# A graph-attention layer on one core: V's slice with its first two score blocks together, another order of V's products, and row statistics at other slots

## The chip, the core and the metric

The kernel runs on one core of one Trainium2 chip. The metric is the device time of one execution in microseconds; the time given for a kernel is the median of its runs. One further execution was recorded by the hardware profiler, and all rows of a profile below come from such a recorded execution.

The engines are named as the profile names them: PE is TensorE's matmuls, PEld its weight loads, DVE is VectorE, ACT is ScalarE, POOL is GpSimd, and SP is the engine from whose queue nearly all transfers are issued.

## The reference

All values are fp32. x is 128 graphs of 128 nodes with 768 features, and adj holds 128 x 128 edge weights per graph, about seven of eight of them zero.

```python
h = relu(layernorm(x))                      # over the 768 features
q, k, v = (split_heads(h @ W + b) for W, b in ((Wq, bq), (Wk, bk), (Wv, bv)))   # 12 heads of 64
scores = q @ k.T / sqrt(64) + beta * adj
scores = where(adj > 0, scores, -9e15)
out = x + merge_heads(softmax(scores) @ v)
```

Each of the 128 graphs attends within itself.

## The kernel before

**Groups and slices.** The graphs go in 32 groups G of four (`GRP`, `NG`). Each group needs three matrix products with the activations of its four graphs: one for Q and K of heads 0 to 5 ("qk0"), one for V ("v"), one for Q and K of heads 6 to 11 ("qk1"). For group 0 they are done plainly (`plain_slice`); for groups 1 to 31 each is a *slice* of 15 products (`slice_z`), by a fast scheme for multiplying 3 x 3 blocks in two rows, and each of the 15 is itself done with seven block products instead of eight (`ZONES`). The loop over G (L1068) writes the work of the three slices into a table `todo` by slot, and `run` (L807) then plays a slice: slot k is the k-th product in the order of `ORDER`. Every engine's instructions run in the order in which this program writes them; nothing reorders them later.

**One product (`product_z`, L531).** It takes 28 matmul instructions (two passes for each of 14), which read one weight tile `T_...` or resident `res_...` and one sum of activations, and write one pair of PSUM banks. There are four pairs. `PRODUCTS` (L66) gives each product a *chain* a, b, c or d. Products of one chain add up in the same pair of banks, in their order, and after each product the pair's content so far is added to one or two results, called homes, named (r, j). So the next product of a chain may write only when the last one's content has been read. A chain takes its pair at its first product and gives it back at its last. For the first products in question:

| product | chain | result (r, j) |
|---|---|---|
| 1 | a | (1, 0), first use |
| 0 | c | (1, 1), first use |
| 3 | b | (1, 0) |
| 5 | a | (0, 0), first use |
| 2 | c | (0, 1), first use |
| 7 | b | (0, 0) |
| 10 | a | (0, 2), first use |
| 6 | c | (0, 2) |
| 13 | a | (1, 2), first use |
| 4 | d | (1, 1) and (1, 2) |
| 8 | d | (1, 0) |

**Reading a pair ("drain").** In V's slice a result's first use is read by VectorE for two of seven blocks (L561) and then ScalarE for five (L562); any later use is one VectorE addition of all seven (L571). After the last use GpSimd turns the home into V's rows (`decode`, L581).

**Scores (L617).** `scores(G, u, j)` writes the scores of two heads for four graphs: 32 matmuls in tiles of another shape (64 x 64), into a pair of its own. It sets its two homes free. At the next slot VectorE adds the mask (L634) and gives the pair back; ScalarE takes the exponential (L636) behind that slot's drain.

**A slot.** `run` writes, in this order: the product's matmuls, then the next weight load (`load_T`, L330, on SP; five buffers, the tile just used is refilled for the fifth streamed product after it); pending masks; the slot's table entries (`then(at, ...)`); what falls due from earlier slots; the product's drain; pending exponentials and divisions; and last the slot's "post" entries.

**Row statistics.** Layernorm's mean and variance of group G+2 are taken while group G is computed, graph by graph (g = 0 to 3): `load_row` (L408) brings the 384 KB of a graph, `row_stats` (L411) sums it and its squares on ScalarE, writing over the buffer (L417 to L419). From group 3 on there is one buffer (`row_home`), so a load waits for the statistics before it, on SP, and all transfers that SP issues later stand behind that wait. The next group's activations are normalised by ScalarE (`norm`, L446, "post" at slots 3, 4, 7, 8 of V's slice), transposed by VectorE (`to_hT`, L459; A11 at slot 10), and summed.

**The order of V's slice before**, with the tables of the change: products 1, 0, 3, 5, 2, 7, 10, 6, 11, 13, 4, 9, 14, 8, 12, in chains a c b a c b a c b a d c b d c. Scores of (u, j) = (0, 2) are at slot 0, (0, 1) at slot 2, (0, 0) at slot 7. Row statistics of g = 1, 2, 3 stand behind slots 1, 5 and 10, the loads of g = 2 and 3 behind slots 2 and 6. In groups 30 and 31 V's slice has no row statistics.

Of the kernel before, what the change touches and what calls it, by code (L numbers as in the profile page):

```python
# [30 lines left out]
@with_exitstack  # L31
def kernel(
    ctx: ExitStack,
    tc: tile.TileContext,
    x: bass.AP,
    adj: bass.AP,
    wq: bass.AP,
    bq: bass.AP,
    wk: bass.AP,
    bk: bass.AP,  # L40
    wv: bass.AP,
    bv: bass.AP,
    beta: bass.AP,
    out: bass.AP,
):

    nc = tc.nc
    keep = ctx.enter_context(tc.tile_pool(name="keep", bufs=1))
    bad = keep.tile([1, 1], I32, name="bad")
    args = (x, adj, wq, bq, wk, bk, wv, bv, beta, out)
    direct(tc, *args, bad)
    again = nc.values_load(bad[0:1, 0:1])
    with tc.If(again > 0):
        general(tc, *args)
# [48 lines left out]

ZORDER = (1, 0, 3, 5, 2, 7, 10, 6, 11, 13, 4, 9, 14, 8, 12)
QORDER = (4, 0, 1, 8, 2, 3, 5, 6, 7, 10, 9, 11, 13, 12, 14)  # L110
LORDER = (1, 4, 0, 8, 5, 2, 10, 3, 6, 7, 13, 9, 11, 12, 14)
ORDER = {"qk0": ZORDER, "v": ZORDER, "qk1": QORDER}
RING = 5
RESIDENT = (3, 8, 12, 16, 20, 25, 29, 33, 35, 38, 41)

# [10 lines left out]
def direct(ctx, tc, x, adj, wq, bq, wk, bk, wv, bv, beta, out, bad):  # L126
# [132 lines left out]

    sequence = [(sl, n) for sl in ("qk0", "v", "qk1") for n in ORDER[sl]]  # L260
    resident = {key: const.tile([P, 7, P], F32, name=f"res_{key[0]}_{key[1]}") for key in (sequence[at] for at in RESIDENT)}
# [61 lines left out]
    def order_of(G, sl):  # L323
        return LORDER if G == NG - 1 and sl == "qk1" else ORDER[sl]

# [135 lines left out]
    def sum_acts(G, name):  # L461
        _, a, b, sign = [row for row in SUMS_A if row[0] == name][0]
        t = full[G, name] = block(SPOT.index(name))
        nc.vector.tensor_tensor(t, full[G, a], full[G, b], ALU.add if sign > 0 else ALU.subtract)
# [66 lines left out]
    def product_z(G, sl, n):  # L531
# [21 lines left out]
        for (r, j), sign in uses:  # L553
# [19 lines left out]
            if not left[key]:  # L573
                last = order_of(G, sl) is LORDER
                engine = nc.vector if sl == "qk1" and (n == 13 or last and n in (11, 12, 14)) else nc.gpsimd
# [240 lines left out]
    def slice_z(G, sl, todo):  # L816
        run([product_z(G, sl, n) for n in order_of(G, sl)], todo)
# [163 lines left out]
    def then(at, f, *args):  # L981
        todo.setdefault(at, []).append(lambda: f(*args))

    def bias(G, *at):
        def go():
            if G not in steps:
                steps[G] = bias_steps(G)
            next(steps[G], None)
        for n in at:
            then(n, go)  # L990

    def attention(G, u, at, behind=5):
        for n, j in at:
            then(n - 3, load_xo, G, 3 * u + j)
            then((n, "post"), attend, G, 3 * u + j, behind)
# [6 lines left out]
    def turn_act(G, slots, behind=0):  # L1002
        for at, name in slots:
            then(at, to_hT, G, int(name[1]), int(name[2]))
            if behind is not None:
                then(at + behind, inner, G, name)

    def sums_at(G, slots):
        for at, name in slots:
            then(at, sum_acts, G, name)  # L1010
# [57 lines left out]
    for G in range(1, NG):  # L1068
        more = G + 1 < NG
        todo.clear()  # L1070
        then(3, scores, G - 1, 1, 2)
        then(5, scores, G - 1, 1, 0)
        then((6, "post"), scores, G - 1, 1, 1)
        attention(G - 1, 1, ((7, 2), (10, 0), (12, 1)))
        sums_at(G, ((0, "S7"), (1, "S0"), (4, "S5"), (7, "S14"), (9, "S11")))
        if G == 1:
            todo[0].insert(0, lambda: sum_acts(1, "S6"))
        if more:
            for g in range(2):
                for h in range(2):  # L1080
                    then((2 * g + h, "post"), norm, G + 1, g, 2 * h, 2 * h + 2)
            turn_act(G + 1, ((8, "A01"), (9, "A00"), (11, "A02")), None)
            then((12, "post"), load_x, G + 1, 1)
            if G + 2 < NG:
                then((7, "post"), row_stats, G + 2, 0)
                then((9, "post"), load_row, G + 2, 1)
        slice_z(G, "qk0", todo)

        todo.clear()
        then(0, scores, G, 0, 2)  # L1090
        then(2, scores, G, 0, 1)
        then(7, scores, G, 0, 0)
        if more:
            then((11, "post"), add_raw, G + 1)
            for n, at in enumerate((3, 4, 7, 8)):
                then((at, "post"), norm, G + 1, 2 + n // 2, n % 2 * 2, n % 2 * 2 + 2)
            turn_act(G + 1, ((10, "A11"),), 1)
            for at, name in ((4, "A01"), (5, "A00"), (6, "A02")):
                then(at, inner, G + 1, name)
            if G + 2 < NG:  # L1100
                for g, at in ((1, 1), (2, 5), (3, 10)):
                    then((at, "post"), row_stats, G + 2, g)
                    if g < 3:
                        then((at + 1, "post"), load_row, G + 2, g + 1)
        slice_z(G, "v", todo)

        todo.clear()
        if not more:
            break
        attention(G, 0, ((3, 2), (9, 1)))  # L1110
        attention(G, 0, ((12, 0),), 6)
        turn_act(G + 1, ((1, "A10"), (4, "A12")), 1)
        sums_at(G + 1, ((6, "S1"), (7, "S9"), (8, "S2"), (11, "S6"), (13, "S10")))
        bias(G + 1, 0, 2, 4)
        if G + 2 < NG:
            then(5, row_moments, G + 2, 6, 9)
            then((6, "post"), load_x, G + 2, 0)
        if G + 3 < NG:
            then((10, "post"), load_row, G + 3, 0)
        slice_z(G, "qk1", todo)  # L1120
# [158 lines left out]
```

## Time and profile before

| | |
|---|---|
| median of three runs | 2706.36 us (2702.01 to 2708.77) |
| the profiled execution | 2712.82 us |
| its span, first to last instruction | 2711.0 us |
| mean granted TensorE clock | 0.996 |
| V's slice, groups 1 to 29, shortest and longest | 26.48 and 30.43 us |
| moved over the span | 721.73 MB, mean 266 GB/s |

The page of the profile gives shares of the span by engine, the chain of work that ended last, and the costliest groups of instructions. The timeline lists instructions in order of time; PE's durations overlap, since a matmul's end is modelled to the end of its pipeline, so the pace of PE is read from one start to the next.

### The profile page before, as it was taken

What the parts mean: (1) busy time and instruction counts of PE and PEld (TensorE: products, weight loads), DVE (VectorE), ACT (ScalarE), POOL (GpSimd) and SP (SyncE); (2) the same over time, 40 slices, a digit from 0 to 9 for tenths busy, and PEclk for the clock granted to TensorE, in tenths of its full rate; (3) what the DMA queues carried; (4) which work ended last, traced back from release to release, by engine and by line L of the source; (5) the groups of instructions that cost most, each with busy time, mean ns of one, the idle gap of its engine ahead of it and who ended that gap; (6) DMA issues with size and microseconds to landing.
All of it is one profiled execution on the core that took longest, in us unless ns stands there. A gap on an engine that the chain in (4) does not pass through costs nothing.

```text
span 2711.0 us, 121562 instructions
## 1 busy us (share of the span) xinstructions
PE 2674.2 (99%) x52029; PEld 2568.3 (95%) x52029; DVE 2188.4 (81%) x2705; ACT 1762.5 (65%) x4612; POOL 2096.0 (77%) x3034
## 2 busy tenths in 40 slices
PE   8999999999999999999999999999999999999997
PEld 7799999999999999999999999999999999999997
DVE  6878888788888788888788878788887888877885
ACT  2476666677666677666767666776666776667653
POOL 4867878777878877888778787778787778887783
PEclk9999999999999999999999999999999999999999
DMA  8789889899889898889899889898898988888875
GB/s 229 262 260 278 274 271 274 259 281 276 271 264 281 260 287 272 271 278 277 259 277 276 275 274 268 269 273 269 270 283 260 280 272 269 280 269 256 253 235 158
DMA packets 530342, 721.73 MB, mean 266 GB/s; under 512 B 105980, under 2 KB 374024, under 8 KB 529800
## 3 DMA queue, kind: packets, MB, share of 16 engines
q1 hardware_dynamic: 528640, 713.12, 86.4%
q8 instruction: 412, 6.75, 1.0%
q10 hardware_dynamic: 1160, 0.79, 0.1%
q14 instruction: 130, 1.06, 0.1%
HBM read 647.73 MB, written 66.05 MB: 263 GB/s over the span
## 4 chain that ended last, share of the span: by engine, by line
PE 87%; POOL 4%; DVE 3%; ACT 2%; DMA 1%; issue 1%; POOLq 0%; DVEq 0%; ACTq 0%
PE pair L547 74%; PE pair L626 7%; PE pair L683 6%; DMA sbig<-in_x_dram 1%; DVE home L571 1%; POOL home L590 1%; POOL home L589 1%; POOL home L592 1%; ACT sbig L419 0%; POOL home L591 0%; ACT sbig L417 0%; ACT home L562 0%; DVE e L634 0%; DVE prep_v L304 0%; ACT e L636 0%
## 5 line engine op out<-in xcount | busy, mean ns | idle before, releaser
L571 DVE TENSOR_TENSOR home<-home,pair 128x896 f32<-128x896 f32 x810 | 860.2, 1075 | 234.2 <-PE pair L547 130.4
L547 PE MATMUL pair<-sbig,T_qk 128*64 128x128 f32 x13888 | 888.6, 274 | 4.1 <-ACT e L666 3.1
L547 PEld LDWEIGHTS pair<-sbig,T_qk 128*64 128x64 f32 x13888 | 758.0, 137 | 17.8 <-issue 8.0
L666 ACT ACTIVATE e<-e,sm 128x64 f32<-128x64 f32 x1512 | 382.2, 341 | 123.5 <-DVE sm L654 123.2
L547 PE MATMUL pair<-A,T_qk 128*64 128x128 f32 x6076 | 415.1, 273 | 0.0
L547 PE MATMUL pair<-T_v,sbig 128*64 128x128 f32 x6944 | 414.2, 274 | 0.3 <-ACT home L562 0.3
L589 POOL TENSOR_TENSOR home<-home 128x256 f32<-128x256 f32 x297 | 227.2, 765 | 237.0 <-DVE home L571 237.0
L683 PE MATMUL pair<-v,e 128*64 128x65 f32 x6048 | 401.8, 221 | 0.0
L565 ACT ACTIVATE home<-pair 128x640 f32<-128x640 f32 x325 | 229.2, 705 | 261.5 <-PE pair L547 196.8
L547 PEld LDWEIGHTS pair<-T_v,sbig 128*64 128x64 f32 x6944 | 385.4, 137 | 6.3 <-issue 4.3
L683 PEld LDWEIGHTS pair<-v,e 128*64 128x64 f32 x6048 | 359.5, 137 | 3.6 <-DVE e L634 0.3
L547 PEld LDWEIGHTS pair<-A,T_qk 128*64 128x64 f32 x6076 | 331.7, 137 | 5.5 <-issue 5.5
L634 DVE SCALAR_TENSOR_TENSOR e<-pair,biasT 128x1024 f32<-128x1024 f32 x189 | 230.4, 1219 | 82.1 <-PE pair L626 82.0
L592 POOL TENSOR_TENSOR home<-home 128x256 f32<-128x256 f32 x297 | 276.3, 930 | 23.3
L590 POOL TENSOR_TENSOR home<-home 128x256 f32<-128x256 f32 x297 | 250.1, 842 | 23.3
L636 ACT ACTIVATE e<-e 128x1024 f32<-128x1024 f32 x189 | 200.2, 1059 | 64.7 <-DVE e L634 56.7
L446 ACT ACTIVATE x<-x,block 128x192 f32<-128x192 f32 x480 | 231.7, 540 | 0.0
L692 ACT ACTIVATE sm<-pair,tiny 128x8 f32<-128x8 f32 x189 | 49.3, 261 | 261.6 <-PE pair L683 261.6
L591 POOL TENSOR_TENSOR home<-home 128x128 f32<-128x128 f32 x297 | 196.9, 663 | 23.3
L547 PE MATMUL pair<-sbig,res_qk 128*64 128x128 f32 x3472 | 211.9, 273 | 0.0
L567 ACT ACTIVATE home<-pair,bqk 128x128 f32<-128x128 f32 x650 | 203.6, 374 | 0.0
L626 PE MATMUL pair<-home 64*64 64x128 f32 x5312 | 196.2, 277 | 6.3 <-issue 4.8
(192 smaller groups left out, 4699.9 us busy)
## 6 DMA issues: line engine op xcount, KB each, us to landing
T_qk<-kept_qk SPq DMA_DIRECT2D x713, 448.0 KB, 4.8
T_v<-kept_v SPq DMA_DIRECT2D x341, 448.0 KB, 4.9
xo<-in_x_dram SPq DMA_DIRECT2D x189, 256.0 KB, 4.5
out_dram<-xo SPq DMA_DIRECT2D x189, 256.0 KB, 5.9
x<-in_x_dram SPq DMA_DIRECT2D x248, 192.0 KB, 6.6
sbig<-in_x_dram SPq DMA_DIRECT2D x116, 384.0 KB, 6.5
kept_qk<-prep_qk SPq DMA_DIRECT2D x23, 448.0 KB, 2.9
adj<-in_adj_dram SPq DMA_DIRECT2D x128, 64.0 KB, 3.9
```

The source lines that it names most:

```text
L446: nc.scalar.activation(t, t, AF.Relu, bias=shift[G, n], scale=rstd[G, n])
L547: nc.tensor.matmul(p[q:q + HD, at, :], lhs[:, q:q + HD], rhs, start=(first and at % 4 == 0), stop=True, skip_group_check=True)
L565: nc.scalar.activation(t[:, 0:5], p[:, 0:5], AF.Copy, scale=float(sign))
L567: nc.scalar.activation(t[:, at], p[:, at], AF.Identity, bias=bqk[:, of, oc:oc + 1], scale=float(sign))
L571: nc.vector.tensor_tensor(t, t, p[:, 0:7], op)
L589: e.tensor_tensor(t[:, 1:4:2], t[:, 1:4:2], twice(5), ALU.add)
L590: e.tensor_tensor(t[:, 2:5:2], t[:, 2:5:2], twice(1), ALU.add)
L592: e.tensor_tensor(t[:, 0:7:6], t[:, 0:7:6], twice(2), ALU.add)
L626: nc.tensor.matmul(ps[k:k + HD, i, g * N:(g + 1) * N], keys[r, k:k + HD], queries[r], start=True, stop=True)
L634: nc.vector.scalar_tensor_tensor(e, ps, SCORE_CAP * ISCALE, bias, op0=ALU.min, op1=ALU.add)
L666: nc.scalar.activation(o[:, r, b, 0:HD], pa[:, r, b, 0:HD], AF.Copy, scale=t[:, 1, r, b:b + 1])
L683: nc.tensor.matmul(pa[q:q + HD, 2 * g + i, :], k[:, q:q + HD], vt[G, "v", r, h // 4][:, 4 * g + h % 4, :], start=True, stop=True, skip_gro ...
```

## The change

Three edits. V's slice gets an order of its own, in which product 3 goes from slot 2 to slot 4, and products 5 and 2 each come one slot sooner; its chains are then a c a c b b a c b a d c b d c. The score block (0, 2) goes from slot 0 to slot 2, where it is written ahead of (0, 1). The statistics of graphs 1 and 2 of group G+2 go from behind slots 1 and 5 to behind slots 4 and 6 (those of graph 3 stay at 10); the load of graph 2 goes from behind slot 2 to behind slot 4, and that of graph 3 from 6 to 7. The same weight tiles stay resident, since the products at those places are the same.

```diff
 ZORDER = (1, 0, 3, 5, 2, 7, 10, 6, 11, 13, 4, 9, 14, 8, 12)
 QORDER = (4, 0, 1, 8, 2, 3, 5, 6, 7, 10, 9, 11, 13, 12, 14)
+VORDER = (1, 0, 5, 2, 3, 7, 10, 6, 11, 13, 4, 9, 14, 8, 12)
...
-ORDER = {"qk0": ZORDER, "v": ZORDER, "qk1": QORDER}
+ORDER = {"qk0": ZORDER, "v": VORDER, "qk1": QORDER}
...
         todo.clear()
-        then(0, scores, G, 0, 2)
+        then(2, scores, G, 0, 2)
         then(2, scores, G, 0, 1)
         then(7, scores, G, 0, 0)
...
             if G + 2 < NG:
-                for g, at in ((1, 1), (2, 5), (3, 10)):
+                for g, at in ((1, 4), (2, 6), (3, 10)):
                     then((at, "post"), row_stats, G + 2, g)
                     if g < 3:
-                        then((at + 1, "post"), load_row, G + 2, g + 1)
+                        then((at + (g == 2), "post"), load_row, G + 2, g + 1)
         slice_z(G, "v", todo)
```

## The prediction

> **What bounds the kernel now.** I read the page first: the share of the span by engine, then the chain that ended last.
>
> ```profile
> span 2711.0 us, 121562 instructions
> PE 2674.2 (99%) x52029; PEld 2568.3 (95%) x52029; DVE 2188.4 (81%) x2705; ACT 1762.5 (65%) x4612; POOL 2096.0 (77%) x3034
> PE 87%; POOL 4%; DVE 3%; ACT 2%; DMA 1%; issue 1%; POOLq 0%; DVEq 0%; ACTq 0%
> ```
>
> TensorE is the bound: whatever makes it wait adds to the time, and what the other engines do is free as long as it lies under its matmuls. So I went on to the timeline of one V slice on each engine. The columns are start, duration, engine, line, operation, tiles and count; in brackets the idle time before and what ended it.
>
> ```profile
> 1312.59 1.70 PE L547 MATMUL pair<-T_v,sbig 128*64 128x128 f32 x28
> 1314.22 1.10 PE L626 MATMUL pair<-home 64*64 64x128 f32 x32
> 1315.26 1.75 PE L547 MATMUL pair<-res_v,sbig 128*64 128x128 f32 x28
> 1316.84 1.70 PE L547 MATMUL pair<-T_v,sbig 128*64 128x128 f32 x28
> ...
> 1332.28 1.75 PE L547 MATMUL pair<-res_v,A 128*64 128x128 f32 x28 [0.51 <-DVE e L634]
> ...
> 1338.54 1.70 PE L547 MATMUL pair<-res_v,A 128*64 128x128 f32 x28
> 1340.07 1.70 PE L547 MATMUL pair<-A,T_qk 128*64 128x128 f32 x28
> ```
>
> A product is one row of 28 matmuls and takes 1.53 us (1338.54 to 1340.07); a block of scores is a row of 32 and takes 1.04 us (1314.22 to 1315.26), with 0.10 us ahead of it (1312.59 + 1.53 = 1314.12) and 0.05 behind it (1315.26 to 1316.84 is 1.58). This slice lasts 27.48 us. One wait stands in it: product 4, at slot 10, waits 0.51 us for the mask of the third block.
>
> The same slice of every group with row statistics (groups 1 to 29), cut from its first product to the next slice's, stands in the view of windows (length, busy time and count of PE, PEld, DVE, ACT and POOL, then granted clock, DMA share, GB/s).
>
> ```profile
> 1890.40:1916.88 26.48, 26.48 (x522) 25.45 (x518) 18.56 (x23) 18.36 (x40) 21.76 (x37) 1.00 0.91 272
> 2466.00:2496.43 30.43, 28.57 (x520) 27.29 (x518) 18.91 (x23) 18.55 (x40) 21.90 (x37) 0.94 0.91 251
> sum 786.89, PE 776.32 PEld 740.98 DVE 539.20 ACT 534.60 POOL 626.92; mean PE 26.77 PEld 25.55 DVE 18.59 ACT 18.43 POOL 21.62
> ```
>
> An undisturbed slice takes 26.48 us; the mean is 786.89 / 29 = 27.13 us. So V's slices hold at most 0.65 us each, 19 us in all, that a better order could take back, beside what the change does to the matmuls themselves.
>
> **The change, part by part.** Times are now counted from the first matmul of V's slice. Slot k is the k-th product.
>
> *One entry into scores less.* Two blocks in a row share one 0.10 us ahead and one 0.05 us behind: 0.15 us saved, less what one block costs behind another (0 to 0.10 us); I take 0.10 us a group. Slots 0, 1, 2 start at 0, 1.53, 3.06; the scores run from 4.69 to 6.77; slot 3 starts at 6.82.
>
> *Chain a at slots 0 and 2 (before: 0 and 3).* A product adds to the pair of banks that its chain's last product was drained from, so it waits for that drain. The last slice shows what it costs to come two slots after: its fourth product stands two behind the one that shares its chain.
>
> ```profile
> 2663.24 1.70 PE L547 MATMUL pair<-sbig,T_qk 128*64 128x128 f32 x28
> 2665.84 0.44 PE L547 MATMUL pair<-A,res_qk 128*64 128x128 f32 x4 [0.90 <-ACT home L567]
> ```
>
> There the drain is longer. V's slot 0 is drained by VectorE and then ScalarE, which ends at 1314.87 + 0.71 - 1312.59 = 2.99 (row below); from the mask's end to the waiting product was 0.06 us (1331.00 + 1.22 = 1332.22 against 1332.28, next fence). So slot 2 could start at 3.05, and PE gets there at 3.06. Cost nothing, hidden by slot 1's matmuls with no margin; the bounds are 0 and 0.4 us (if ScalarE comes late by the 0.38 us it idles there now). I take 0. Chain c, at 1 and 3, has the two blocks between: nothing.
>
> *Chain b at slots 4 and 5 (before: 2 and 5).* This is the first real cost. Product 3 is now drained while nothing but product 7 is queued on PE, and product 7 is of the same chain.
>
> ```profile
> 1318.65 1.09 DVE L571 TENSOR_TENSOR home<-home,pair 128x896 f32<-128x896 f32 x1 [0.18 <-PE pair L547]
> ...
> 1321.37 0.42 DVE L561 TENSOR_TENSOR home<-bv_b,pair 128x256 f32<-128x256 f32 x1 [0.49 <-PE pair L547]
> ...
> 1330.00 1.09 DVE L571 TENSOR_TENSOR home<-home,pair 128x896 f32<-128x896 f32 x1 [3.63 <-ACT home L562]
> 1331.00 1.22 DVE L634 SCALAR_TENSOR_TENSOR e<-pair,biasT 128x1024 f32<-128x1024 f32 x1
> ...
> 1334.22 0.71 DVE L459 STREAM_TRANSPOSE A<-x 128x512 f32<-128x512 f32 x1 [0.68 <-ACT x L446]
> 1334.86 5.04 DVE L571 TENSOR_TENSOR home<-home,pair 128x896 f32<-128x896 f32 x5
> ```
>
> Product 3's own drain of before starts 1.81 us after its product (1316.84 to 1318.65) and takes 1.09; with 0.06 to PE that is 2.96 us, against 1.53 of product: 1.43 us of PE idle in each of 31 groups. VectorE is free for it: the second mask ends near 8.2, slot 3's part near 9.1, and slot 4 is done only at 10.2. Slot 5 starts at 8.35 + 2.96 = 11.31. Undisturbed, the slice now takes 26.48 - 0.10 + 1.43 = 27.8 us, its slot 13 starts 3.06 before the end, at 24.7.
>
> *Row statistics at 4, 6, 10 instead of 1, 5, 10; loads at 4 and 7 instead of 2 and 6.* All groups 3 and up share one row buffer, so this is a ring: statistics, load, statistics. ScalarE's timeline of before has the prices, and SP's the load.
>
> ```profile
> 1314.87 0.71 ACT L562 ACTIVATE home<-pair 128x640 f32<-128x640 f32 x1 [0.38 <-DVE home L561]
> ...
> 1319.13 0.83 ACT L417 ACTIVATE sbig<-sbig 128x768 f32<-128x768 f32 x1
> ...
> 1321.82 0.70 ACT L562 ACTIVATE home<-pair 128x640 f32<-128x640 f32 x1 [0.47 <-DVE home L561]
> 1322.42 1.05 ACT L636 ACTIVATE e<-e 128x1024 f32<-128x1024 f32 x1
> 1323.37 0.98 ACT L446 ACTIVATE x<-x,block 128x192 f32<-128x192 f32 x2
> 1324.24 0.69 ACT L562 ACTIVATE home<-pair 128x640 f32<-128x640 f32 x1
> ...
> 1327.14 0.84 ACT L417 ACTIVATE sbig<-sbig 128x768 f32<-128x768 f32 x1 [1.34 <-DMA sbig<-in_x_dram]
> ...
> 1329.28 0.68 ACT L562 ACTIVATE home<-pair 128x640 f32<-128x640 f32 x1
> ```
> ```profile
> 1321.37 0.33 SPq L409 DMA_DIRECT2D sbig<-in_x_dram  x1
> ```
>
> Now row 1 starts at 6.54 and its successor's load is issued at 8.78 (2.24 us later). In the new order ScalarE does, from slot 3 on: its drain, which starts 0.45 us behind VectorE's start (1321.37, 1321.82), and that 1.87 us behind the second product of a pair begun at 1319.50, so at 6.82 + 2.32 = 9.14; then 0.60 drain, two exponentials of 0.95, two pairs of norms of 0.87, and 2.24 of row 1: the load of row 2 goes out at 9.14 + 0.60 + 1.90 + 1.74 + 2.24 = 15.6, 6.9 us later than now. Row 2's statistics stand only two slots on, and ScalarE reaches them at 16.3, behind slot 6's drain.
>
> How long the load takes from issue to its reader: 5.77 us here, where ScalarE waited for it (1321.37 to 1327.14). The undisturbed group bounds it from the other side.
>
> ```profile
> 1903.47 0.84 ACT L417 ACTIVATE sbig<-sbig 128x768 f32<-128x768 f32 x1
> ```
> ```profile
> 1899.14 0.33 SPq L409 DMA_DIRECT2D sbig<-in_x_dram  x1
> ```
> ```profile
> L335 SPq DMA_DIRECT2D T_v<-kept_v x7: 319/323/392, 1312.8 to 1329.8; - x7
> ...
> DMA to landing us min/median/max: 3.3/4.9/6.6
> ```
>
> There it took at most 4.33 us, with no wait. The fastest of the larger weight transfers (448 KB against 384) landed in 3.3. In the new place SP itself stands at this load's wait from about 10.0 to 15.6, so what it issued earlier has landed and the load goes out alone: I take 3.8 us, between 3.3 and 4.33; the bounds are 3.3 and 5.8.
>
> Then everything behind it on ScalarE is late: row 2 starts at 19.4; 2.14 to its successor (1327.14 to 1329.28), norms 0.87, the third exponential 0.95, norms 0.87: 24.3. VectorE's transpose of A11 needs these norms and stands ahead of slot 10's two drains: 0.04 + 0.64, then two of 1.01 (5.04 for five), then 0.06 to PE: 27.1. Slot 13 (product 8) is of product 4's chain, d, and waits for both. PE is there at 24.7: **2.4 us of stall**, and the slice ends at 27.1 + 3.06 = 30.2. The formula is 26.4 plus the load's time; the cover is gone from 1.4 us of load time on, and no row is that short.
>
> SP's queue: slot 6's weight load waits from 14.4 to 15.7, and those of slots 8, 9 and 11 stand behind row 3's load, which waits for row 2 until 21.7. With five buffers they are the next slice's first three, due at 30.2: some 6.9 us or more, against 4.9 in the landing row; hidden. The adjacency load behind them goes the same way. GpSimd's decodes follow the drains and keep their distance to the slice's end. What row 2 gives back: it no longer stands ahead of slot 6's drain, so the 0.51 us of slot 10 is gone; that is in the 27.13 already.
>
> *The clock.* One group of before shows what a gap of this size does besides.
>
> ```profile
> 2474.82 0.44 PE L626 MATMUL pair<-home 64*64 64x128 f32 x6 [1.86 <-issue]
> 2475.19 4.94 PE L547 MATMUL pair<-T_v,sbig 128*64 128x128 f32 x56
> ```
> ```profile
> 2476.00:2477.00 1.00, 1.00 (x14) 1.00 (x12) 0.53 (x1) 0.00 (x0) 0.92 (x2) 0.50 0.96 308
> ```
> ```profile
> 1814.99 0.59 PE L626 MATMUL pair<-home 64*64 64x128 f32 x10 [1.39 <-issue]
> ```
>
> Behind 1.86 us of idle the granted clock fell to 0.50 and two products took 4.94 us instead of 3.28 (row of 56 at full clock: 1.70 + 1.53 and 0.05): 1.66 us more. Behind 1.39 us another group shows no such row. So 1.43 us at slot 5 should leave the clock alone, and 2.4 us at slot 13 should cost it, in most groups; from 0 to 1.66 us each I take 1.16, seven groups in ten. By the Trainium skill (TensorE: Matmul & The Clock Gate, "What's actually happening") the clock falls after an idle window of about 3.4 us; by that, 2.4 us would cost nothing and the sum would be 34 us less. The row at 1.86 us disagrees.
>
> **The sum,** against this execution's own 2712.82 us: 29 groups at 30.2 - 27.13 = 3.07 us are 89; two last groups without row statistics at 1.43 - 0.10 are 3; the clock, 29 at 1.16, is 34. Together 126 us. The profiled run stands 6.5 us above the median of the three, 2706.36, so the forecast for the median is 2832 us.
>
> **The rivals.**
> - *The clock holds.* The same two stalls, but at slot 13 no drop: 2706 + 92 = 2798 us. For it speaks the 1.39 us row, against it the 1.86 us one. The page on the clock gate is on its side.
> - *The row's wait is covered.* ScalarE's idle time swallows it, or row 1 is done earlier than I count, and only slot 5 is left: 29 times 27.8 - 27.13 and the 3 are 22 us, 2728. It needs the load to be at its reader 1.4 us after issue, or row 1 some 2.4 us sooner; the landing rows speak against both.
> - *The load is slow and the clock always falls.* At 5.8 us the slice takes 32.2: 29 times 5.07 and the 3 are 150, the clock 48: 2904. For it: the load took 5.77 with the queues full.
> - *Faster.* Product 7 isn't held by product 3's drain, because other work of PE or a shorter hand-over fills slot 5, and row 2, gone from slot 6's drain, frees slot 10: the slice falls to 26.4, 29 times 0.75 saved, 2684. Slot 5 decides: from 0.75 us of gap on the gain is eaten. Against it stands 1.09 us for the drain alone.
>
> **How the numbers follow.** Forecast 0.52, the clock holds 0.22, slow load 0.13, covered 0.08, faster 0.05. About 0.3% (8 us) can be told from no change here; every case but the last is above it: slower 0.94, same 0.01, faster 0.05. The range is 2760 (a load of 2.5 us, the clock full: 28.9 us, 51 + 3) to 2890 (5.3 us with the clock falling each time): it leaves out the covered case, the faster one and the slowest end.
>
> **What would show it.** Slot 5 with a wait of about 1.4 us put down to VectorE's drain L571; product 8 at slot 13 with one of about 2.4 us on the same line; row 2's statistics with some 3 us of wait for the transfer of x in every group, and row 3's not before 25; granted clock of 0.50 behind slot 13; V's slice near 31 us, the other two slices unchanged. Wrong if slot 5 starts as its predecessor ends, if L417 shows no waits for its transfer, or if the loss sits in another slice.

## The result, and the profile after

The changed kernel takes 2783.94 us (median of six runs, 2782.45 to 2787.64) against 2705.24 us for the kernel before (six runs as well). The ratio is 1.0288, 95% interval 1.0274 to 1.0301: slower by 79 us. The forecast was 2832 us, range 2760 to 2890. Its direction and the places of both waits were right; the loss was 79 us where it said 126, because the second wait was shorter and the lower clock did not come.

The page of the changed kernel, as shown of before: the span, the share of each engine, and the chain that ended last. A line was added ahead of the functions, so line numbers of before are one higher here (L547 is L548).

```profile
span 2780.7 us, 121472 instructions
PE 2671.7 (96%) x52029; PEld 2563.4 (92%) x52029; DVE 2183.2 (79%) x2705; ACT 1766.9 (64%) x4612; POOL 2100.7 (76%) x3034
PE 69%; DMA 10%; ACT 9%; DVE 5%; POOL 2%; issue 1%; SPq 1%; ACTq 0%; POOLq 0%; DVEq 0%
```

PE has the same matmuls and nearly the same busy time, but its share of the chain fell from 87% to 69%: transfers, ScalarE and VectorE are now on the path. Where, PE's timeline of one V slice shows (group 15, start, duration, engine, line, operation, count; in brackets the wait and what ended it).

```profile
1345.82 1.70 PE L548 MATMUL pair<-T_v,sbig 128*64 128x128 f32 x28
...
1348.87 1.72 PE L548 MATMUL pair<-T_v,sbig 128*64 128x128 f32 x28
1350.53 1.98 PE L627 MATMUL pair<-home 64*64 64x128 f32 x64
1352.43 3.32 PE L548 MATMUL pair<-T_v,sbig 128*64 128x128 f32 x56
1356.93 1.75 PE L548 MATMUL pair<-res_v,sbig 128*64 128x128 f32 x28 [1.18 <-DVE home L572]
...
1367.34 3.23 PE L548 MATMUL pair<-T_v,sbig 128*64 128x128 f32 x56
1372.05 1.75 PE L548 MATMUL pair<-T_v,A 128*64 128x128 f32 x28 [1.49 <-DVE home L572]
1373.63 1.70 PE L548 MATMUL pair<-res_v,A 128*64 128x128 f32 x28
1375.16 1.70 PE L548 MATMUL pair<-A,T_qk 128*64 128x128 f32 x28
```

Both waits stand where they were forecast and name VectorE's drain: product 7 at slot 5 and product 8 at slot 13. The first row of 56 holds slots 3 and 4. In the kernel before, two such products behind a block of scores take 3.11 us:

```profile
1319.50 3.28 PE L547 MATMUL pair<-T_v,sbig 128*64 128x128 f32 x56
1322.61 1.70 PE L547 MATMUL pair<-res_v,sbig 128*64 128x128 f32 x28
```

Here slot 5 starts 4.50 us behind the row's start (1352.43 to 1356.93), so 1.39 us are lost; in 27 of the 31 slices slot 5 starts 2.89 us behind slot 4, which is 1.36 us more than a product. The bracket says 1.18, since a matmul's modelled end lies behind the next one's possible start: a loss is read from start to start. By the same reading slot 13 loses 1.65 us (1367.34 to 1372.05 is 4.71, two products are 3.06), where its bracket says 1.49.

The ring of the row statistics behind the second wait, on ScalarE, SP and VectorE in the same slice:

```profile
1359.07 0.83 ACT L418 ACTIVATE sbig<-sbig 128x768 f32<-128x768 f32 x1
...
1364.35 0.85 ACT L418 ACTIVATE sbig<-sbig 128x768 f32<-128x768 f32 x1 [2.48 <-DMA sbig<-in_x_dram]
```
```profile
1361.31 0.33 SPq L410 DMA_DIRECT2D sbig<-in_x_dram  x1
```
```profile
1369.32 0.71 DVE L460 STREAM_TRANSPOSE A<-x 128x512 f32<-128x512 f32 x1 [2.80 <-DMA sbig<-in_x_dram]
1369.95 5.04 DVE L572 TENSOR_TENSOR home<-home,pair 128x896 f32<-128x896 f32 x5
```

Row 1 starts at 1359.07, 13.25 us into the slice; row 2's load goes out at 15.49 and reaches its reader 3.04 us later; VectorE's transpose, which stands ahead of slot 10's two drains, starts at 23.5; the second drain ends near 1372.0, and slot 13 starts at 1372.05. In the waits of the whole execution (who waited for whom, us in total, times, longest) the ring is a large entry. The first line is of the kernel before, the others of the changed one; the last two lines together are the 31 waits at slot 5 and the 29 at slot 13.

```profile
ACT sbig L417 <- DMA sbig<-in_x_dram: 8.7, 10, 1.7
ACT sbig L418 <- DMA sbig<-in_x_dram: 81.1, 43, 3.1
...
PE pair L548 <- DVE home L572: 65.9, 50, 2.1
PE pair L548 <- DVE sbig L572: 13.7, 10, 2.1
```

V's slices of groups 1 to 29 in the view of windows (length; busy time and count of PE, PEld, DVE, ACT, POOL; granted clock, DMA share, GB/s):

```profile
1345.82:1375.16 29.34, 26.67 (x521) 25.46 (x518) 18.22 (x23) 18.62 (x40) 21.41 (x36) 1.00 0.83 247
...
sum 856.12, PE 775.30 PEld 738.15 DVE 529.81 ACT 538.84 POOL 620.40; mean PE 26.73 PEld 25.45 DVE 18.27 ACT 18.58 POOL 21.39
```

The mean is 856.12 / 29 = 29.52 us against 27.13. That is 69.2 us more in the 29 slices; the two last slices, without row statistics, take 27.61 each, 2.2 us more together. The spans differ by 69.7 us: the whole loss sits in V's slices. No slice shows a granted clock below 1.00.

### The profile page after: what moved, and what is told of

It is laid out like the page before. It is cut to its first block, busy times and chain, and to the rows that moved or that the text cites. A ratio compares the mean times of both kernels' runs of the same rounds, so it can differ in the third digit from the quotient of the medians.

```text
span 2780.7 us, 121472 instructions
## 1 busy us (share of the span) xinstructions
PE 2671.7 (96%) x52029; PEld 2563.4 (92%) x52029; DVE 2183.2 (79%) x2705; ACT 1766.9 (64%) x4612; POOL 2100.7 (76%) x3034
## 4 chain that ended last, share of the span: by engine, by line
PE 69%; DMA 10%; ACT 9%; DVE 5%; POOL 2%; issue 1%; SPq 1%; ACTq 0%; POOLq 0%; DVEq 0%
PE pair L548 59%; PE pair L684 6%; DMA sbig<-in_x_dram 5%; PE pair L627 4%; DMA out_dram<-xo 3%; DVE home L572 2%; ACT e L637 2%; ACT x L447 2%; ACT sbig L420 2%; ACT sbig L418 2%; DMA T_qk<-kept_qk 1%; DVE A L460 1%; ACT strow L419 0%; DMA x<-in_x_dram 0%; POOL home L591 0%
## 5 line engine op out<-in xcount | busy, mean ns | idle before, releaser
L548 PE MATMUL pair<-sbig,T_qk 128*64 128x128 f32 x13888 | 885.2, 273 | 4.9 <-DMA T_qk<-kept_qk 4.1
L548 PEld LDWEIGHTS pair<-sbig,T_qk 128*64 128x64 f32 x13888 | 754.0, 137 | 19.3 <-issue 9.7
L548 PE MATMUL pair<-T_v,sbig 128*64 128x128 f32 x6944 | 414.4, 273 | 2.2 <-issue 2.0
L548 PE MATMUL pair<-A,T_qk 128*64 128x128 f32 x6076 | 414.8, 273 | 0.0
L590 POOL TENSOR_TENSOR home<-home 128x256 f32<-128x256 f32 x297 | 237.8, 801 | 227.4 <-DVE home L572 219.7
L548 PEld LDWEIGHTS pair<-T_v,sbig 128*64 128x64 f32 x6944 | 382.5, 137 | 10.0 <-issue 8.0
L566 ACT ACTIVATE home<-pair 128x640 f32<-128x640 f32 x325 | 229.2, 705 | 238.2 <-PE pair L548 177.3
L548 PEld LDWEIGHTS pair<-A,T_qk 128*64 128x64 f32 x6076 | 330.6, 137 | 5.5 <-issue 5.5
L593 POOL TENSOR_TENSOR home<-home 128x256 f32<-128x256 f32 x297 | 276.3, 930 | 23.3
L591 POOL TENSOR_TENSOR home<-home 128x256 f32<-128x256 f32 x297 | 274.8, 925 | 23.3
L470 POOL TENSOR_TENSOR A<-A 128x256 f32<-128x256 f32 x186 | 156.6, 842 | 120.2 <-DVE A L460 120.2
L548 PE MATMUL pair<-sbig,res_qk 128*64 128x128 f32 x3472 | 211.7, 273 | 0.0
L637 ACT ACTIVATE e<-e 128x1024 f32<-128x1024 f32 x189 | 196.2, 1056 | 23.5 <-DVE e L635 15.7
L563 ACT ACTIVATE home<-pair 128x640 f32<-128x640 f32 x160 | 111.6, 698 | 143.9 <-DVE home L562 143.9
```

Of the source, the lines that this page charges most:

```text
L548: nc.tensor.matmul(p[q:q + HD, at, :], lhs[:, q:q + HD], rhs, start=(first and at % 4 == 0), stop=True, skip_group_check=True)
L566: nc.scalar.activation(t[:, 0:5], p[:, 0:5], AF.Copy, scale=float(sign))
L590: e.tensor_tensor(t[:, 1:4:2], t[:, 1:4:2], twice(5), ALU.add)
L591: e.tensor_tensor(t[:, 2:5:2], t[:, 2:5:2], twice(1), ALU.add)
L593: e.tensor_tensor(t[:, 0:7:6], t[:, 0:7:6], twice(2), ALU.add)
L637: trailing.append(lambda: nc.scalar.activation(e, e, AF.Exp, scale=1.0 / ISCALE))
```

## The experiments

Each kernel was run beside the kernel before on the same chip; ratios are against that, with 95% intervals. What is not in a diff is as in the kernel that it starts from.

### The statistics put back

From the changed kernel:

```diff
-                for g, at in ((1, 4), (2, 6), (3, 10)):
+                for g, at in ((1, 1), (2, 5), (3, 10)):
...
-                        then((at + (g == 2), "post"), load_row, G + 2, g + 1)
+                        then((at + 1, "post"), load_row, G + 2, g + 1)
```

> The changed kernel with the row statistics and their loads at the slots of before (1, 5, 10 and 2, 6); V's order and the score blocks stay changed. Theory (two separate terms: product 7 waits for product 3's drain at slot 5; the ring statistics, load, statistics makes slot 13 late): the wait of slot 13 is gone in every group, that of slot 5 stays at about 1.2 us of PE idle, V's slice takes about 27.6 to 27.9 us, in all 2720 to 2735 us. Rival (the order and the scores cost it all, the statistics nothing): V's slice stays at 29.4 us and the time at 2775 to 2785.

2734.76 us, ratio 1.0106 (1.0082 to 1.0131). No slice waits at slot 13; every one of the 31 waits at slot 5 (the two lines of waits below, 26 and 5 times). Then two rows of the windows and their sum:

```profile
PE pair L548 <- DVE home L572: 30.9, 26, 1.2
...
PE pair L548 <- DVE sbig L572: 6.0, 5, 1.2
```

```profile
1407.05:1434.65 27.60, 26.41 (x521) 25.44 (x519) 18.40 (x23) 18.50 (x40) 22.08 (x37) 1.00 0.90 269
1489.65:1517.25 27.60, 26.41 (x520) 25.44 (x518) 18.39 (x23) 18.50 (x40) 22.05 (x37) 1.00 0.91 269
...
sum 817.16, PE 772.48 PEld 741.45 DVE 535.35 ACT 536.64 POOL 639.59; mean PE 26.64 PEld 25.57 DVE 18.46 ACT 18.50 POOL 22.05
```

An undisturbed slice takes 27.60 us. The order and the scores alone cost 29 us; the rival, that they cost it all, is out.

### The statistics alone

The kernel before, with the two changed lines of the row statistics.

> The kernel before with only the row statistics and their loads at the new slots. Theory: no wait at slot 5, but the load of row 2 goes out at 15.4 us in the slice and its reader gets it 2.9 us later, so slot 13 can start at 25.9 us, where PE now arrives at 23.4: a stall of some 2.3 us instead of 1.4, slice about 29.0 us, in all 2755 to 2765 us if the clock holds; if gaps of more than 2 us bring the clock down as one of 1.9 us did in the kernel before, up to 48 us more, 2800 to 2810. So the two parts don't add up: the statistics alone cost 50 to 60, though they add only about that much on top of the order too. Rival (the statistics hurt only because the order puts the exponentials and drains in their way): about 2705.

2798.19 us, ratio 1.0356 (1.0329 to 1.0382): more than the whole change, and just under the 2800 to 2810 us expected where the clock falls. The wait at slot 13 is 2.2 to 2.7 us (in the brackets) in all 29 slices, and the granted clock of a slice falls in 19 of them. PE's timeline and the windows by single microseconds around one such wait, then the windows by slice:

```profile
1372.27 3.23 PE L547 MATMUL pair<-T_v,sbig 128*64 128x128 f32 x56
1377.88 3.25 PE L547 MATMUL pair<-T_v,A 128*64 128x128 f32 x28 [2.38 <-DVE home L571]
```
```profile
1378.00:1379.00 1.00, 1.00 (x10) 1.00 (x12) 1.00 (x2) 0.00 (x0) 0.92 (x3) 0.50 0.96 370
```
```profile
1351.90:1382.62 30.72, 28.34 (x521) 27.06 (x518) 18.61 (x23) 18.39 (x40) 22.82 (x39) 0.94 0.85 254
1437.62:1466.49 28.87, 26.70 (x520) 25.43 (x518) 18.50 (x23) 18.39 (x40) 21.31 (x36) 1.00 0.84 253
```

The second of the slices, with its clock at 1.00, lasts 28.87 us, near what the ring's sum has (29.0). The first lasts 1.85 us longer: 1.63 of it from slot 13 on, where one product took 3.25 us instead of 1.70, and the rest in a longer wait. The ten slices at full clock last 29.23 us in the mean, 2.1 more than the mean slice before, and the 19 others 30.81. So of the 91 us that the V slices of the two profiled executions differ by, about 61 are the wait (29 times 2.1) and about 30 the clock that it brings down (19 times 1.58).

### The changed kernel without two loads

```diff
-                        then((at + (g == 2), "post"), load_row, G + 2, g + 1)
+                        pass
```

> The changed kernel without the loads of rows 2 and 3 in V's slice; the statistics of these graphs are taken over what the buffer holds, so the output's later groups are normalised by other numbers. All instructions of ScalarE, VectorE and PE stay. Theory (it is the load's time that makes slot 13 late, not ScalarE's work): row 2 starts right behind slot 6's drain, slot 13 has no wait, V's slice takes about 27.6 us, 2725 to 2735 us. Rival (ScalarE has too much to do between slots 3 and 9, and the load is hidden behind it): slot 13 still waits more than 0.8 us, 2760 or more. The removed 768 KB a group of 22 MB are too little to matter otherwise.

2733.23 us, ratio 1.0104 (1.0083 to 1.0124). ScalarE does all its work at the same places, row 2 right behind slot 6's drain, and slot 13 starts as slot 12 ends:

```profile
1343.73 0.68 ACT L563 ACTIVATE home<-pair 128x640 f32<-128x640 f32 x1
1344.32 0.83 ACT L418 ACTIVATE sbig<-sbig 128x768 f32<-128x768 f32 x1
```
```profile
1349.88 3.23 PE L548 MATMUL pair<-T_v,sbig 128*64 128x128 f32 x56
1352.94 1.70 PE L548 MATMUL pair<-T_v,A 128*64 128x128 f32 x28
```

It is the load's time that makes slot 13 late, not ScalarE's work.

### The order alone

The changed kernel with the statistics put back and one block of scores at slot 0 again:

```diff
-        then(2, scores, G, 0, 2)
+        then(0, scores, G, 0, 2)
```

> The changed order of V's products alone: the score blocks at slots 0, 2 and 7 and the statistics as before. Theory: slot 5 waits as in the changed kernel; one more entry into the scores' tiles than with both blocks at slot 2 costs 0.1 to 0.3 us a group, so 3 to 9 us more than the kernel with only the statistics put back: 2725 to 2745 us. Rival (the two blocks in a row themselves cost, by the masks and exponentials that come together): 5 us or more below that kernel.

2738.6 us, ratio 1.013 (1.0108 to 1.0153). The medians can't tell it from the kernel with the statistics put back (their intervals overlap); its undisturbed slices can:

```profile
1408.44:1436.33 27.89, 26.70 (x521) 25.43 (x518) 18.91 (x23) 18.61 (x40) 21.98 (x37) 1.00 0.88 262
1491.52:1519.41 27.89, 26.70 (x520) 25.43 (x518) 18.91 (x23) 18.64 (x40) 21.98 (x37) 1.00 0.86 256
```

27.89 against 27.60 us: the second block behind the first saves 0.29 us in a slice without other waits, the one thing in the change that gains. In the sum over 29 slices of the two profiled executions the gain doesn't show (814.87 us here, 817.16 with both blocks at slot 2), where PE's waits put down to "issue" come to 10.4 us with both blocks together and to 2.4 here. Whether the blocks in a row bring these waits wasn't tried.

### Chain b apart

From the changed kernel, with the statistics put back:

```diff
-VORDER = (1, 0, 5, 2, 3, 7, 10, 6, 11, 13, 4, 9, 14, 8, 12)
+VORDER = (1, 0, 5, 2, 3, 10, 7, 6, 11, 13, 4, 9, 14, 8, 12)
```

> Both score blocks at slot 2 as in the changed kernel, row statistics as before, and V's products 7 and 10 change places (1, 0, 5, 2, 3, 10, 7, 6, ...), so that chain b comes at slots 4 and 6. Theory (the loss of the order is the missing product between 3 and 7, and nothing else): product 3's drain takes 2.96 us from its product's start, two products 3.06, so the wait is gone; an undisturbed slice takes 27.60 - 1.43 = 26.2 us against 26.48 before, 0.3 us a group for the entry into the scores that is saved: 2690 to 2700 us, faster than before by 5 to 15. Rival (the two score blocks in a row cost by their masks, or the pair of chain b comes late): a wait at slot 4 or 6 of 0.5 us or more, 2715 us or more.

2690.35 us, ratio 0.9941 (0.9924 to 0.9958): 0.6% faster than before. One other product between 3 and 7 is enough:

```profile
1387.04:1413.23 26.19, 26.19 (x521) 25.46 (x518) 18.39 (x23) 18.46 (x40) 22.11 (x37) 1.00 0.94 283
1468.44:1494.64 26.20, 26.20 (x521) 25.47 (x519) 18.40 (x23) 18.47 (x40) 22.11 (x37) 1.00 0.93 279
```

The slice went from 27.60 to 26.19 us, 1.41 us where 1.43 was expected, and PE is busy over all of it.

### Chain b apart, with the changed statistics

The same exchange of 7 and 10 in the changed kernel, nothing else.

> The changed kernel with products 7 and 10 exchanged as in the kernel with chain b apart, and the row statistics at the changed slots. One wait is taken away from the changed kernel, and nothing added. Theory (the ring sets when slot 13 may start, whatever PE does ahead of it, and gaps above some 2.2 us bring the clock down): PE comes to slot 13 sooner by 1.4 us and waits there by as much longer, 2.6 to 3.0 us; the slice without a fall of the clock stays at 29.3 us, and with it takes 31.0 us in at least two groups of three: 2800 to 2835 us, slower than the changed kernel. Rival (the two waits are separate costs that add up): 2784 less 31 times 1.4, about 2740 us.

2799.58 us, ratio 1.0347 (1.0327 to 1.0367). It has one wait less than the changed kernel, and is slower by 16 us. PE reaches slot 13 sooner and stands there longer:

```profile
1377.68 3.23 PE L548 MATMUL pair<-T_v,sbig 128*64 128x128 f32 x56
1383.81 3.25 PE L548 MATMUL pair<-T_v,A 128*64 128x128 f32 x28 [2.90 <-DVE home L572]
```

The waits lie between 2.3 and 3.1 us, and 15 of 29 slices show a lower clock; the expectation had at least two in three, and 2800 us or more. Slot 13 starts 26.20 us into this slice (1357.61 to 1383.81) and 26.23 us into the one of the changed kernel: the ring sets its time, whatever PE does ahead of it. Costs that add up would have given 2740.

### Row 2 at slot 6, its load left at slot 2

Two kernels: the one with chain b apart, and the kernel before, each with row 2's statistics behind slot 6 and row 3's load behind slot 7.

```diff
-                for g, at in ((1, 1), (2, 5), (3, 10)):
+                for g, at in ((1, 1), (2, 6), (3, 10)):
...
-                        then((at + 1, "post"), load_row, G + 2, g + 1)
+                        then(((0, 2, 7)[g], "post"), load_row, G + 2, g + 1)
```

> The kernel with chain b apart, and of the row statistics only row 2's go from slot 5 to slot 6 with row 3's load at slot 7; row 1 and row 2's load stay at 1 and 2. Theory: row 2's load keeps its 6 us ahead of its reader; nothing waits for it. The same time as the kernel with chain b apart within 5 us, 2688 to 2700. Rival (slot 6 as such is too late for row 2): a wait at slot 13 and 2720 us or more.

2688.53 us, ratio 0.994 (0.9924 to 0.9956): the same as with chain b apart. It is the fastest median seen, but not to be told from that kernel.

> The kernel before with only row 2's statistics from slot 5 to slot 6, row 3's load from 6 to 7. Theory: row 2, where it waits for its load, no longer stands ahead of slot 6's drain, so slot 10's waits for the mask (0.2 to 0.5 us in some six groups, 3 us in all) go: 2700 to 2706 us, hardly to be told from before. Rival (the later slot alone makes slot 13 late): 2720 us or more.

2697.45 us, ratio 0.9975 (0.9966 to 0.9984). The gain is small, but more than the 2700 to 2706 us expected. The waits for the mask at slot 10 are gone. Their price had been set by the brackets, which is too low: the slice of before with a bracket of 0.51 us lasted 27.48 us where an undisturbed one lasts 26.48. So slot 6 for row 2 is no fault; its load's place was.

## Why the prediction was right, and where it was off

- **Chain b at slots 4 and 5**: right in place, cause and size. From product 3's start to product 7's 2.96 us were worked out, and 2.89 measured. The stall of 1.43 us is 1.36, and the product behind the stall starts 0.05 us later than usual (1356.93 to 1358.51 is 1.58). The exchange of 7 and 10 took away 1.41.
- **Chain a at slots 0 and 2**: no cost, as taken. The third product starts 3.05 us into the slice, and the slices of 26.19 us with the same start have no wait.
- **One entry into scores less**: 0.10 us taken, 0.29 measured in undisturbed slices. Two blocks in one row take 1.90 us (1350.53 to 1352.43); two single ones 2.08, and each has its own entry besides. Part of a single block's 1.04 us may be its entry; no run parts the two.
- **The ring**: right in place and cause. Row 2's load goes out 15.5 us into the slice (15.6 forecast). The term that was mis-sized is the load's time: 3.8 us taken, and 2.94 measured as the median over the 29 slices from the load's issue to row 2's first instruction. The lower bound of 3.3 us came from larger transfers that shared the queues with others. This load met queues that had run dry (DMA share 0.92 two microseconds before its issue, 0.00 in the 0.69 us behind it), though two weight loads follow it within 1 us, so the bound didn't hold for it. Slot 13 lost 1.65 us in the slice shown where 2.4 were forecast. The working's own formula, 26.4 us plus the load's time, gives 29.34 with the median of 2.94, against 29.52 us for the mean slice; with the 3.04 us of the slice shown it gives 29.44, and that slice lasts 29.34. By the Trainium skill (DMA: Bandwidth & Descriptors, "Anatomy of one DMA — SWDGE (gpsimd) path") a transfer issued from GpSimd takes about 2.0 us and its bytes at 436 GB/s, an estimate of 2.9 us for these 393,216 bytes. The 2.94 us measured agree, though this load goes out on SP's queue.
- **The clock**: 34 us taken, none measured, so the case that had the largest chance didn't come. Waits of 2.2 us and more did bring the clock down in 19 of 29 slices with the statistics alone, near the seven in ten taken. In the changed kernel the wait is mostly 1.2 to 1.8 us in the brackets, because the load came 0.9 us sooner. The working also set the 2.4 us of slot 13, a loss from start to start, beside gaps of 1.86 and 1.39 us that were read from brackets, and it took the length of a gap for what decides; the last section shows that it isn't.
- **The whole**: between the profiled executions the loss is 69.7 us where the sum said 126, 56 us less. Of these, 29 times 0.86 for the load is 25, and the clock is 34; small disturbances, 0.18 us a slice above the formula, give 5 back, and the two last slices and the rest of the execution took some 2.5 less than summed. (Between the medians the loss is 79 us, since the profiled execution of before was 7.6 us above the median of six and that of the changed kernel 1.4 below.) The range held the time because its lower end was worked out with a full clock and a short load; it doesn't bear out the clock's 34 us.
- **The rivals**: "the clock holds" (2798 us) came nearest. "Covered" is refuted by the 81.1 us of waits for the load, "faster" by slot 5; but its mechanism, other work of PE in slot 5's gap, is what made the faster kernel.

What stays open: waits put down to "issue", up to 2.2 us, mostly in or behind the score blocks of slot 2. They come in all kernels, mostly in other groups each time, and make the mean slice some 0.2 to 0.65 us longer than the undisturbed one where slot 13 doesn't wait. Their cause wasn't tried.

## What to carry to other kernels

Read a chain of products by the gap between two of the same accumulator: the drain's start, its length and the hand-over must fit under the products in between, here 2.89 us under two of 1.53. When work around one buffer is a ring (use, load, use), moving one use moves the load behind it and everything queued behind its next reader; look for the engine whose queue then stands, and follow it to the next matmul. Waits in series on one path don't add up: the later one can take up what the earlier one leaves, so taking away the wrong one first can lose.

## What the runs showed of the hardware

Within the slices the granted TensorE clock fell to half for 3.41 us at a time (twice for 6.83), and all falls of one execution start on one beat of 3.41 us: with the statistics alone, those at 1377.84 and 1548.51 us are 50 beats apart. A fall costs some 1.7 us beside the wait, half of a beat. What brings it about is how much of one beat PE idles, not how long the wait is. Below are beats of two waits in the view of windows (length, then busy time of PE first; the granted clock is third from the end). The first two rows are of the statistics alone, around the wait of 2.38 us shown above; the other three are of chain b apart with the changed statistics, around a wait of 2.88 us that ended at 613.13.

```profile
1374.43:1377.84 3.41, 1.07 (x20) 0.82 (x16) 2.69 (x4) 3.32 (x8) 1.65 (x3) 1.00 0.96 296
1377.84:1381.26 3.42, 3.38 (x32) 3.38 (x34) 2.06 (x3) 0.00 (x0) 3.20 (x7) 0.50 1.07 250
```
```profile
608.20:611.61 3.41, 2.05 (x38) 1.81 (x34) 1.21 (x2) 3.41 (x7) 0.42 (x1) 1.00 0.82 261
611.61:615.03 3.42, 1.90 (x34) 1.90 (x36) 3.42 (x5) 1.40 (x5) 2.93 (x7) 1.00 1.07 318
615.03:618.44 3.41, 3.41 (x68) 3.41 (x66) 3.02 (x5) 0.39 (x1) 3.25 (x7) 1.00 0.89 285
```

The shorter wait left PE idle for 2.34 us of one beat, and the next beat ran at half clock. The longer one fell into two beats, 1.36 and 1.52 us, and the clock stayed. In these two executions every one of the 34 beats with 2.08 us of idle PE or more was followed by a fall, and none of those with up to 2.01 us. In the other kernels three falls came behind beats with 1.73, 1.86 and 1.93 us, and beats with 1.89 and 1.91 us passed without one, so what decides between 1.7 and 2.0 us stays open. In the changed kernel the waits of up to 2.10 us left at most 1.75 us idle in any beat. The 15 falls with chain b apart and the changed statistics, some 25 us, are more than the 16 us by which that kernel is slower than the changed one.
